# Turning the layer norms by VectorE and DMA instead of TensorE in a macaron transformer block

## The chip, the core and the metric

The kernel runs on one core of a Trainium2 chip. The core has a matrix engine (TensorE, PE in the profile; its weight loads are PEld), a vector engine (VectorE, DVE), a scalar engine (ScalarE, ACT), GpSimd (POOL) and SyncE (SP), which here issues most of the DMAs. Every engine works through its own list of instructions in order and waits for semaphores where it needs another engine's result. The metric is the time of one execution on the device in microseconds; lower is better.

## The reference

The input x is 2 sequences of 1024 rows with 1024 features. Three residual steps follow each other: half a feed-forward layer, an attention layer, and the same half feed-forward layer again, each of them applied to a layer norm of x.

```python
x = x + 0.5 * ffn(layernorm(x))        # gate_w, base_w, base_b, lora_A, lora_B
x = x + attn(layernorm(x))             # Wq, Wk, Wv, Wo
x = x + 0.5 * ffn(layernorm(x))        # the same weights as the first
```

`layernorm` subtracts the mean of a row and divides by its standard deviation. `ffn(h)` is `h @ base_w.T + base_b` plus a low-rank part: 8 experts of rank 16, of which each row uses the best 2 by `h @ gate_w.T`, with softmax weights. `attn(h)` has 32 query heads and 8 key/value heads of width 32, rotary positions, a causal mask and a softmax in fp32, and ends in `ctx @ Wo`.

## The kernel before

The 2048 rows are cut into 16 tiles of 128 rows, eight for each sequence. A tile passes five kinds of stages: a1 (first feed-forward), a2 (queries, keys, values), the attention itself in units of one tile and one key/value head, c1 (output projection) and c2 (second feed-forward). Python generators (`stage_a1`, `stage_a2`, `stage_c1`, `stage_c2`) emit the dense work in pieces, and `step(s)` mixes the pieces of several tiles with the attention units of tile s by a table written by hand (`NORMAL`, `SEQS`). The order in which the instructions finally stand on each engine is then set by a scheduler that plays the program against a timeline of its own.

Matrix products are made at more than fp16 precision by splitting both sides into a high and a low fp16 half; `dense` multiplies high by high, high by low and low by high (lines L406, L407, L408). Its left side must have the features on the partitions, but a layer norm works with rows on the partitions. So every layer norm ends with a turn (a transpose) of a 128 by 1024 tile into `c.tt`, which holds 8 blocks of the high half and 8 of the low half. There are three layer norms for each tile, 48 in all.

`layernorm(xt, turn)` takes the statistics on VectorE, and then ScalarE writes the normalised tile `xn` in fp32 (L397). With `turn=True`, `turn_rows` transposes the fp32 tile by eight TensorE transposes and splits it on the way out of PSUM; that holds for the first two layer norms of the tiles 0 to 2, six cases. In the other 42 cases `turn_halves` first makes the high half on ScalarE (L355) and the low half on VectorE (L357), each 128 by 1024 fp16 in `hl`, and puts two closures into the list `later`. Each closure calls `turned8`: eight TensorE transposes of 128 by 128 into one of the three PSUM buffers `s` (L332), and a copy to `c.tt` on ScalarE (L333). `tick()` is called once for each slot of attention (one block of keys for one head, `unit_s2`); it counts the entries down and runs the first one that is due, `TLAG` slots after it was put there. If a consumer comes earlier, `dense` calls `tt.settle()`, which runs what is left at once.

The same three buffers `s` hold the scores of the first pass (L649, with their maxima on VectorE, L666), and `turned8` also turns queries and keys. The second pass makes the scores again (L782), ScalarE takes the exponential (L788), and TensorE forms the sums with the values (L727).

SP issues in one order: the streamed weights (`prefetch`, 1 MB each, `ws<-wstr`, L418) into three buffers, the rows of maxima that go into the queries (four small DMAs for each pair of heads, `qt<-mt`, L685), the inputs and the outputs (L136, L821). GpSimd issues the DMA that adds the bias to `xt` (L444), once `xn` has been read from it.

Of the kernel before, what the change touches and what calls it, by code (L numbers as in the profile page):

```python
# [9 lines left out]
FP = mybir.dt.float32  # L10
HP = mybir.dt.float16
I32 = mybir.dt.int32
AF = mybir.ActivationFunctionType
ALU = mybir.AluOpType
# [3 lines left out]
NH, NKV, DH, GRP = 32, 8, 32, 4  # L18
E, R = 8, 16
P = 128  # L20
KB = D // P
NT = B * T // P
# [5 lines left out]
LATE = TPB  # L28
# [5 lines left out]
NEARLY = 3  # L34
LOFF = 2
NTURN, NTURN2 = 3, 3
TLAG = 12
SB, LB = 3, 2


# [1 line left out]
def kernel(  # L42
# [16 lines left out]
    nc = tc.nc  # L59
# [5 lines left out]
    small = ctx.enter_context(tc.tile_pool(name="small", bufs=SB))  # L65
    xp = ctx.enter_context(tc.tile_pool(name="xp", bufs=5))
    fpool = ctx.enter_context(tc.tile_pool(name="f32", bufs=1))
    hlp = ctx.enter_context(tc.tile_pool(name="hl", bufs=2))
    tp = ctx.enter_context(tc.tile_pool(name="tp", bufs=4))
    dram = ctx.enter_context(tc.tile_pool(name="dram", bufs=1, space=bass.MemoryType.DRAM))  # L70
    p_dense = ctx.enter_context(tc.tile_pool(name="p_dense", bufs=2, space=bass.MemoryType.PSUM))
# [16 lines left out]
        out=cmask, in_=cmask, compare_op=ALU.is_ge, fill=-NEG, base=0,  # L88
# [6 lines left out]
        out=tri, in_=tri, compare_op=ALU.is_gt, fill=0.0, base=0,  # L95
# [8 lines left out]
    MR = 3 * DH  # L104
    MC = 2
    W = DH
    G = P // W
# [15 lines left out]
    xts, Ts = {}, {}  # L123
# [203 lines left out]
    def turned8(out, src, rows):  # L327

        ps = p_s1.tile([P, GRP, P], FP, name="s1").rearrange("p h k -> p (h k)").bitcast(HP)
        ps = ps.rearrange("p (b q) -> p b q", q=P)  # L330
        for b in range(8):
            nc.tensor.transpose(ps[0:rows, b, :], src[:, b, 0:rows], ident16)  # L332
        nc.scalar.copy(out, ps[0:rows])  # L333

    later = deque()
# [4 lines left out]
    def tick():  # L340
# [3 lines left out]
        if later and later[0][0] <= 0:  # L344
            do_later()

    def turn_halves(xn):

        c = Halves()
        hl = hlp.tile([P, 2 * KB, P], HP, name="hl")  # L350
        for n in range(2):
            h = hl[:, n * KB : (n + 1) * KB, :]
            hi = hl[:, 0:KB, :].rearrange("p k c -> p (k c)")
            if n == 0:
                nc.scalar.copy(hi, xn)  # L355
            else:
                nc.vector.tensor_tensor(h.rearrange("p k c -> p (k c)"), xn, hi, ALU.subtract)  # L357

            def turn(n=n, h=h):
                turned8(c.tt[:, n * KB : (n + 1) * KB, :], h, P)  # L360
                c.todo -= 1

            c.todo += 1
            later.append([TLAG + n, turn])
        return c

    def turn_rows(xn):
# [11 lines left out]
    def layernorm(xt, turn=False):  # L379
        st = small.tile([P, 2, 6], FP, name="bst")  # L380
        for c in range(2):
            nc.vector.bn_stats(st[:, c, :], xt[:, bass.ts(c, 512)])  # L382
        mv = small.tile([P, 2], FP, name="mv")
        nc.vector.bn_aggr(mv, st.rearrange("p a b -> p (a b)"))
        ve = small.tile([P, 1], FP, name="ve")
        nc.gpsimd.tensor_scalar(ve, mv[:, 1:2], EPS, None, ALU.add)
        r = small.tile([P, 1], FP, name="r")
        nc.gpsimd.tensor_tensor(r, ve, mhalf, ALU.pow)
        n1 = small.tile([P, 1], FP, name="n1")
        nc.vector.scalar_tensor_tensor(n1, ve, r, r, ALU.mult, ALU.mult)  # L390
        nc.vector.tensor_scalar(n1, n1, -0.5 * XS, 1.5 * XS, ALU.mult, ALU.add)
        rs = small.tile([P, 1], FP, name="rs")
        nc.vector.tensor_tensor(rs, n1, r, ALU.mult)
        nb = small.tile([P, 1], FP, name="nb")
        nc.vector.scalar_tensor_tensor(nb, mv[:, 0:1], -1.0, rs, ALU.mult, ALU.mult)
        xn = fpool.tile([P, D], FP, name="xn")
        nc.scalar.activation(xn, xt, AF.Identity, bias=nb, scale=rs)  # L397
        return turn_rows(xn) if turn else turn_halves(xn)

    def dense(ps, tt, wsel, n=512, last=True):  # L400
# [11 lines left out]
    turn = [2]  # L412
# [221 lines left out]
    def unit_s1(t, g):  # L634

        b0 = t - t % TPB
        L = t - b0 + 1
        odd = g % 2
        if not odd:
            Ts["mx"] = small.tile([P, 2, TPB, GRP], FP, name="mx", bufs=1)  # L640
        mx = Ts["mx"]
        q = Ts["q1", (t, g - odd)][:, odd * GRP : (odd + 1) * GRP, :]
        for j in reversed(range(L)):
            ps = p_s1.tile([P, GRP, P], FP, name="s1")
            diag = j == L - 1
            off = diag and L > LOFF
            pem = diag and not off
            for h in range(GRP):
                nc.tensor.matmul(  # L649
                    ps[:, h, :], lhsT=q[0 : 3 * DH, h, :], rhs=KT[b0 + j][0 : 3 * DH, g, :],  # L650
                    start=(not pem or h == 0), stop=not pem,
                )
            if pem:
                nc.tensor.matmul(
                    ps, lhsT=negid, rhs=cmask.unsqueeze(1).to_broadcast([P, GRP, P]),
                    start=False, stop=True,
                )
            if off:
                sm = pp.tile([P, GRP, P], FP, name="sm", bufs=1)
                nc.scalar.copy(sm, ps)  # L660
                nc.gpsimd.affine_select(  # L661
                    out=sm, in_=sm, compare_op=ALU.is_ge, fill=-3.0e38, base=0,
                    pattern=[[0, GRP], [-1, P]], channel_multiplier=1,
                )
                ps = sm
            nc.vector.tensor_reduce(mx[:, odd, j, :], ps, AX.X, ALU.max)  # L666
            yield
        if not odd:
            return
        q1 = Ts.pop(("q1", (t, g - 1)))  # L670
        if L > 1:
            m = small.tile([P, 2, GRP], FP, name="m4")
            nc.vector.tensor_reduce(m, mx[:, :, 0:L, :].rearrange("p a j h -> p a h j"), AX.X, ALU.max)
        else:
            m = mx[:, :, 0, :]

        mm = mms[g // 2 % 2]
        mi = mm[:, 0 : 4 * GRP].rearrange("p (i a h) -> p i a h", i=2, a=2)
        nc.vector.tensor_scalar(mi[:, 0], m, 1.0 / MROW, None, ALU.mult)
        nc.vector.scalar_tensor_tensor(mi[:, 1], m, 1.0 / MROW, mi[:, 0], ALU.mult, ALU.subtract)  # L680
        mt = small.tile([P, W], HP, name="mt")
        nc.vector.transpose(mt, mm)
        row = q1[MR : MR + MC].rearrange("i h (a r) -> i a h r", r=W)
        for a in range(G):
            nc.sync.dma_start(out=row[:, a], in_=mt[a * W : a * W + 4 * GRP])  # L685
        Ts["q2", t, g - 1] = q1

    pend = deque()
# [109 lines left out]
    def stage_c1(t):  # L798
        while t not in CT:
            av_batch()  # L800
        tt = CT.pop(t)
        xt = xts[t]
        for n in range(2):
            ps = p_dense.tile([P, 512], FP, name="pd")
            yield from dense_streamed(ps, tt, 3 + n)
            c = bass.ts(n, 512)
            nc.vector.scalar_tensor_tensor(xt[:, c], ps, S["uo", n], xt[:, c], ALU.mult, ALU.add)
            if n == 0:
                yield True
        Ts["x3", t] = layernorm(xt)  # L810
        yield True

    def stage_c2(t):
# [312 lines left out]
```

## Time and profile before

| | |
|---|---|
| time before, median of 3 runs | 1580.93 us (1577.99 to 1581.23) |
| time of the profiled execution | 1578.13 us |
| its span, first to last instruction | 1576.3 us |
| mean granted clock of TensorE | 0.983 |
| busy: TensorE, VectorE, ScalarE, GpSimd | 94%, 71%, 57%, 24% |
| transposes of layer norm halves, L332 | 672 |
| their copies out of PSUM, L333 | 84 of 1019 ns |
| moved by DMA | 214.25 MB, mean 136 GB/s |

A line of the groups reads: line of the kernel, engine, operation, tile written and tiles read, shapes and count; then the busy time of the group in us and the mean of one in ns; then the engine's idle time just before, and what ended it. Busy time counts overlapping instructions once. A matmul's duration is its latency from start to end; the next one can start long before that.

### The profile page before, as it was taken

The numbers are of one execution on the slowest core, as the hardware profiler recorded it, in microseconds if no ns is written. First come the engines' busy times: TensorE is split into PE (matmuls) and PEld (weight loads), VectorE is DVE, ScalarE is ACT, GpSimd is POOL, SyncE is SP. The second block draws the span as 40 slices with busy tenths as digits, with TensorE's granted clock in tenths as the row PEclk, the third lists the DMA queues.
The fourth block names the chain that finished last, engine by engine and source line by source line (L and its number), as shares of the span: only waits on it lengthen the run. The fifth ranks groups of instructions, "written<-read, shape, count | busy, mean of one in ns | idle before, by whom it ended". The sixth has DMA issues, their size and how long they took to land.

```text
span 1576.3 us, 38332 instructions
## 1 busy us (share of the span) xinstructions
PE 1488.0 (94%) x15908; PEld 865.4 (55%) x15908; DVE 1120.9 (71%) x2454; ACT 893.6 (57%) x1523; POOL 381.0 (24%) x636
## 2 busy tenths in 40 slices
PE   5898999999999999989999898999999999999998
PEld 3345556555565555656554454655555556566644
DVE  6777668757587686787744575766869688689653
ACT  8575546556466465565642545554746556566731
POOL 3342333222132231221211122222222122221120
PEclk9998999999999999999999999999999999999999
DMA  8943163262522603513526324345170431601241
GB/s 292 327 134 135 55 227 109 70 249 57 216 95 91 232 14 122 189 42 138 188 76 251 121 95 161 122 156 167 44 277 17 181 129 31 248 27 69 82 161 41
DMA packets 57501, 214.25 MB, mean 136 GB/s; under 512 B 19952, under 2 KB 23024, under 8 KB 37872
## 3 DMA queue, kind: packets, MB, share of 16 engines
q1 hardware_dynamic: 51248, 184.54, 32.6%
q0 software_dynamic: 4640, 16.78, 5.8%
q10 hardware_dynamic: 1440, 10.49, 1.6%
q8 instruction: 125, 2.05, 0.5%
q14 instruction: 48, 0.39, 0.1%
HBM read 191.34 MB, written 20.19 MB: 134 GB/s over the span
## 4 chain that ended last, share of the span: by engine, by line
PE 74%; DVE 11%; ACT 7%; issue 2%; DMA 2%; POOL 1%; SPq 0%; DVEq 0%; ACTq 0%; POOLq 0%
PE pd L406 14%; PE pd L407 14%; PE pd L408 14%; PE av L727 11%; PE s L782 6%; PE s L649 6%; DVE mx L666 3%; PE s L332 3%; ACT p L788 2%; DVE bst L382 1%; DMA ws<-wstr 1%; DVE pair L706 1%; DVE o L736 1%; ACT tt L333 1%; DVE ws L208 1%
## 5 line engine op out<-in xcount | busy, mean ns | idle before, releaser
L788 ACT ACTIVATE p<-s,cs 128x512 f32<-128x512 f32 x576 | 378.0, 690 | 163.5 <-PE s L782 160.8
L666 DVE TENSOR_REDUCE mx<-s 128x4 f32<-128x512 f32 x480 | 313.9, 674 | 80.1 <-PE s L649 70.3
L706 DVE TENSOR_TENSOR pair<-p,p 128x512 f32<-128x512 f32 x256 | 178.9, 701 | 80.9 <-ACT p L788 31.4
L782 PE MATMUL s<-qt,kts 98*128 98x512 f16 x576 | 207.4, 387 | 16.8 <-ACT p L788 9.5
L649 PE MATMUL s<-kts,qt 96*128 96x128 f16 x2304 | 210.3, 223 | 11.2 <-DVE mx L666 8.3
L406 PE MATMUL pd<-ws,tt 128*128 128x512 f16 x544 | 206.4, 380 | 2.5 <-DMA ws<-wstr 1.0
L649 PEld LDWEIGHTS <-qt 96*128 96x128 f16 x2304 | 161.4, 99 | 85.4 <-issue 39.9
L407 PE MATMUL pd<-ws,tt 128*128 128x512 f16 x544 | 206.1, 379 | 0.0
L408 PE MATMUL pd<-ws,tt 128*128 128x512 f16 x544 | 205.3, 379 | 0.0
L406 PE MATMUL pd<-wb,tt 128*128 128x512 f16 x512 | 197.8, 386 | 6.3 <-DVE xt L493 4.9
L407 PE MATMUL pd<-wb,tt 128*128 128x512 f16 x512 | 197.1, 385 | 1.3 <-DVE wb L208 1.3
L408 PEld LDWEIGHTS <-tt 128*128 128x128 f16 x1312 | 128.7, 98 | 125.9 <-issue 7.8
L407 PEld LDWEIGHTS <-tt 128*128 128x128 f16 x1312 | 129.5, 99 | 122.3 <-issue 14.3
L408 PE MATMUL pd<-wb,tt 128*128 128x512 f16 x512 | 196.4, 384 | 0.0
L406 PEld LDWEIGHTS <-tt 128*128 128x128 f16 x1312 | 129.0, 99 | 122.1 <-issue 11.3
L727 PE MATMUL av<-p,va 128*32 128x128 f32 x4608 | 167.2, 278 | 5.1 <-POOL p L790 3.8
L727 PEld LDWEIGHTS av<-p,va 128*32 128x32 f32 x4608 | 115.2, 110 | 74.4 <-issue 50.7
L743 POOL TENSOR_TENSOR tt<-o,tt 128x128 f16<-128x128 f32 x128 | 61.3, 479 | 372.3 <-ACT tt L742 366.0
L790 POOL TENSOR_SCALAR_AFFINE_SELECT p<-p 128x512 f32<-128x512 f32 x128 | 82.6, 647 | 260.4 <-ACT p L788 256.4
L736 DVE RECIPROCAL o<-o 128x128 f32<-128x128 f32 x128 | 120.5, 942 | 22.9 <-ACT o L734 22.7
L661 POOL TENSOR_SCALAR_AFFINE_SELECT sm<-sm 128x512 f32<-128x512 f32 x96 | 71.1, 741 | 229.0 <-ACT sm L660 218.6
L333 ACT COPY tt<-s 128x1024 f16<-128x1024 f16 x84 | 84.3, 1019 | 34.3 <-PE s L332 33.8
(203 smaller groups left out, 2175.0 us busy)
## 6 DMA issues: line engine op xcount, KB each, us to landing
ws<-wstr SPq DMA_DIRECT2D x142, 1024.0 KB
xt<-hb POOLq DMA_DIRECT2D x32, 512.0 KB, 5.5
wstr<-ws ACTq DMA_DIRECT2D x9, 1024.0 KB
xt<-in_x_dram SPq DMA_DIRECT2D x16, 512.0 KB
out_dram<-xt SPq DMA_DIRECT2D x15, 512.0 KB
qt<-mt SPq DMA_DIRECT2D x256, 1.0 KB
ws<-in_wb_dram SPq DMA_DIRECT2D x2, 1024.0 KB
qst<-in_wb_dram SPq DMA_DIRECT2D x2, 1024.0 KB
```

Of the source, the lines that this page charges most:

```text
L333: nc.scalar.copy(out, ps[0:rows])
L406: nc.tensor.matmul(ps, lhsT=th, rhs=wh, start=(k == 0), stop=False)
L407: nc.tensor.matmul(ps, lhsT=th, rhs=wl, start=False, stop=False)
L408: nc.tensor.matmul(ps, lhsT=tl, rhs=wh, start=False, stop=(last and k == KB - 1))
L649: nc.tensor.matmul(ps[:, h, :], lhsT=q[0 : 3 * DH, h, :], rhs=KT[b0 + j][0 : 3 * DH, g, :], start=(not pem or h == 0), stop=not pem,)
L666: nc.vector.tensor_reduce(mx[:, odd, j, :], ps, AX.X, ALU.max)
L706: nc.vector.tensor_tensor(sums, us[i][1], us[i + 1][1], ALU.add)
L727: prev = nc.tensor.matmul(av[rows, i, :], lhsT=w, rhs=p32[:, h, :], start=(us[0][0] == 0 and n == 0), stop=(last and n == len(runs) - 1), ...
L736: nc.vector.reciprocal(rc, rc)
L782: ins = nc.tensor.matmul(ps.rearrange("p h k -> p (h k)"), lhsT=KT[b0 + j][0 : MR + MC, g, :], rhs=q[0 : MR + MC].rearrange("p h k -> p (h ...
L788: nc.scalar.activation(p32, ps, AF.Exp, scale=cs)
L790: nc.gpsimd.affine_select(out=p32, in_=p32, compare_op=ALU.is_ge, fill=0.0, base=0, pattern=[[0, GRP], [1, P]], channel_multiplier=-1,)
```

## The change

Forty of the layer norms are no longer turned by TensorE. VectorE transposes `xn` in fp32, once, in blocks of 32 by 32: inside each group of 32 partitions, 32 rows and 32 features change places. That leaves the rows' groups (`a`, four of them) on the wrong side, and four DMAs, one for each group of 32 partitions, spread 32 partitions of 4 KB over 128 partitions of 1 KB (`xc[:, a]` from `xb[a*32:(a+1)*32]`). For the features to land in order, ScalarE writes `xn` with its features permuted (`xo`, `xi`). The high and the low half are formed from `xc` after the move, directly into `c.tt`, by one ScalarE copy and one VectorE subtraction, as one entry of `later` that is due after 5 slots (`TLAG`) where the two turns were due after 12 and 13. `xb` and `xc` have one buffer each; `hl` is gone. The helper `moved` issues the four DMAs on SP, and the rows of maxima use it too, with the same DMAs as before. The layer norms after attention of tile 15 and tile 8 (`NT - 1` and `LATE`) now go through `turn_rows`. Queries and keys are turned by `turned8` as before.

```diff
-TLAG = 12
+TLAG = 5
...
+    def moved(out, src, rows=W):
+
+        for a in range(G):
+            nc.sync.dma_start(out=out[:, a], in_=src[a * W : a * W + rows])
+
     def turn_halves(xn):
 
         c = Halves()
-        hl = hlp.tile([P, 2 * KB, P], HP, name="hl")
-        for n in range(2):
-            h = hl[:, n * KB : (n + 1) * KB, :]
-            hi = hl[:, 0:KB, :].rearrange("p k c -> p (k c)")
-            if n == 0:
-                nc.scalar.copy(hi, xn)
-            else:
-                nc.vector.tensor_tensor(h.rearrange("p k c -> p (k c)"), xn, hi, ALU.subtract)
-
-            def turn(n=n, h=h):
-                turned8(c.tt[:, n * KB : (n + 1) * KB, :], h, P)
-                c.todo -= 1
-
-            c.todo += 1
-            later.append([TLAG + n, turn])
+        xb = fpool.tile([P, G, KB, W], FP, name="xb")
+        nc.vector.transpose(xb.rearrange("p b k r -> p k b r"), xn.rearrange("p (k b c) -> p k b c", b=G, c=W))
+        xc = fpool.tile([P, G, KB, W], FP, name="xc")
+        moved(xc, xb)
+        hi, lo = [
+            c.tt[:, n * KB : (n + 1) * KB, :].rearrange("p k (a r) -> p k a r", r=W) for n in range(2)
+        ]
+        xk = xc.rearrange("p a k r -> p k a r")
+
+        def halves():
+            nc.scalar.copy(hi, xk)
+            nc.vector.tensor_tensor(lo, xk, hi, ALU.subtract)
+            c.todo = 0
+
+        c.todo = 1
+        later.append([TLAG, halves])
         return c
...
         xn = fpool.tile([P, D], FP, name="xn")
-        nc.scalar.activation(xn, xt, AF.Identity, bias=nb, scale=rs)
+        xo, xi = xn, xt
+        if not turn:
+            xo = xn.rearrange("p (k b c) -> p k c b", b=G, c=W)
+            xi = xt.rearrange("p (k c b) -> p k c b", b=G, c=W)
+        nc.scalar.activation(xo, xi, AF.Identity, bias=nb, scale=rs)
         return turn_rows(xn) if turn else turn_halves(xn)
...
-        row = q1[MR : MR + MC].rearrange("i h (a r) -> i a h r", r=W)
-        for a in range(G):
-            nc.sync.dma_start(out=row[:, a], in_=mt[a * W : a * W + 4 * GRP])
+        moved(q1[MR : MR + MC].rearrange("i h (a r) -> i a h r", r=W), mt, 4 * GRP)
...
-        Ts["x3", t] = layernorm(xt)
+        Ts["x3", t] = layernorm(xt, turn=t in (NT - 1, LATE))
```

More of the change, by code (lines that the diff above doesn't have):

```diff
@@ L67 @@
     fpool = ctx.enter_context(tc.tile_pool(name="f32", bufs=1))
-    hlp = ctx.enter_context(tc.tile_pool(name="hl", bufs=2))
     tp = ctx.enter_context(tc.tile_pool(name="tp", bufs=4))
```

## The prediction

> **What bounds the kernel now.** I read the page's busy shares and chain first, then the groups by line, then TensorE's timeline around one turned tile, the windows of 50 us, and last SP's own issues and waits.
>
> ```profile
> span 1576.3 us, 38332 instructions
> PE 1488.0 (94%) x15908; PEld 865.4 (55%) x15908; DVE 1120.9 (71%) x2454; ACT 893.6 (57%) x1523; POOL 381.0 (24%) x636
> PE 74%; DVE 11%; ACT 7%; issue 2%; DMA 2%; POOL 1%; SPq 0%; DVEq 0%; ACTq 0%; POOLq 0%
> ```
>
> TensorE is busy for 94% of the span and carries 74% of the chain that ended last. What leaves its queue is worth something; what is added elsewhere counts only where it makes TensorE wait.
>
> ```profile
> L333 ACT COPY tt<-s 128x1024 f16<-128x1024 f16 x84 | 84.3, 1019 | 34.3 <-PE s L332 33.8
> L397 ACT ACTIVATE xn<-xt,nb,rs 128x1024 f32<-128x1024 f32 x48 | 59.6, 1243 | 39.1 <-DVE nb L395 32.5 <-DVE hl L357 4.5 <-DVE rs L393 2.0
> L357 DVE TENSOR_TENSOR hl<-xn,hl 128x1024 f16<-128x1024 f32 x42 | 56.5, 1346 | 21.1 <-ACT hl L355 21.0
> L332 PE MATMUL s<-ident,hl 128*128 128x128 f16 x672 | 52.0, 222 | 2.2 <-ACT sm L660 0.9 <-DVE mx L666 0.6 <-ACT tt L742 0.3
> L355 ACT CAST hl<-xn 128x1024 f16<-128x1024 f32 x42 | 43.9, 1046 | 0.5
> L682 DVE STREAM_TRANSPOSE mt<-mm 128x32 f16<-128x32 f16 x64 | 13.0, 203 | 1.3
> ```
>
> These are what the change touches: 42 layer norms, each with 16 transposes on TensorE and two copies out of PSUM on ScalarE. A mean of 222 ns is not what a transpose costs TensorE, because matmuls overlap. The timeline says what it costs: start to next start.
>
> ```profile
> 606.39 0.61 PE L332 MATMUL s<-ident,hl 128*128 128x128 f16 x8
> 606.84 0.39 PE L649 MATMUL s<-kts,qt 96*128 96x128 f16 x4
> 607.06 0.61 PE L332 MATMUL s<-ident,hl 128*128 128x128 f16 x8
> 607.51 0.60 PE L782 MATMUL s<-qt,kts 98*128 98x512 f16 x2
> ```
>
> Eight transposes hold the queue for 0.45 us (606.39 to 606.84, 607.06 to 607.51): 56 ns each, 0.9 us for one layer norm.
>
> ```profile
> 500.00:550.00 50.00, 50.00 (x518) 27.61 (x515) 33.97 (x68) 26.11 (x46) 10.88 (x18) 1.00 0.69 242
> 650.00:700.00 50.00, 45.40 (x622) 28.61 (x623) 44.40 (x92) 32.51 (x55) 12.69 (x20) 0.97 0.21 62
> 1400.00:1450.00 50.00, 50.00 (x769) 33.26 (x768) 45.32 (x92) 33.39 (x59) 9.04 (x14) 0.97 0.11 37
> ```
>
> Columns: busy time of PE, PEld, DVE, ACT, POOL, granted clock, DMA share, GB/s. In most windows TensorE is alone near 50 of 50 and DMA is heavy; where a tile has many keys (650 to 700, 1400 to 1450) VectorE is at 44 to 45 of 50 as well, and DMA is nearly idle.
>
> ```profile
> SPq L685 <- DVE mt L682: 360.0, 43, 24.2
> SPq L418 <- PE pd L408: 280.9, 73, 12.0
> L685 SPq DMA_DIRECT2D qt<-mt x256: 597/610/2811, 121.6 to 1504.7; - x128
> L418 SPq DMA_DIRECT2D ws<-wstr x142: 319/320/453, 118.8 to 1530.7; - x142
> 582.45 1.65 DMA qt<-mt
> 1049.06 4.91 DMA ws<-wstr
> ```
>
> SP issues in order and mostly waits: for VectorE's row of maxima (L685) and for TensorE to free a weight buffer (L418). An issue takes 0.32 us (simple shape) or 0.61 us (three dimensions). The chain has small DMAs at 1.65 us from issue to landing, and runs through a weight load for all its 4.91 us: such a load can arrive just in time.
>
> **The change part by part.** The built order of the two kernels has 40 layer norms in the new form, two (tiles 15 and 8 after attention) moved to the older fp32 form of TensorE, six as before.
>
> *TensorE.* Removed: 42 x 16 x 56 ns = 37.6 us. Added: 2 x 8 fp32 transposes at 8.1/48 = 0.17 us (busy time and count of the group L373 s<-ident,xn), 2.7 us. Net -34.9. The Trainium skill's page TensorE: Matmul & The Clock Gate (Part 4: PE-mode transpose) gives some 275 ns for one in a kernel's context; by that 42 x 16 would be 185 us of queue, and the run would end near 1395. The row's 222 ns agrees with it only as a latency; the starts stand 56 ns apart, and the group's whole busy time is 52.0 us. I take the row.
>
> *The end.* The last layer norm goes xn 1547.4, halves, 16 transposes at 1556.5, copies to 1559.2, and TensorE idles 0.9 us there; the older form is ready sooner. -1.5 us.
>
> *ScalarE.* 84 copies go (-84 us of busy time), the 40 copies for the high half stay (1.05 us each, now read from xc). xn is written with a stride of 32 elements; no row shows such a write. Bounds: 1.24 us as now, or twice that; I take 1.24, as the same count of elements passes. At twice, 40 x 1.24 = 50 us still leave ScalarE below 57%: nothing on the path but POOL's bias add behind xn (L444).
>
> *PSUM.* Turned tiles took 84 turns of the three s buffers that scores (L649), maxima (L666) share. Fewer turns should help, but the scheduler also places everything else anew: -10 to +5 us; I take 0 and keep both ends for the range.
>
> *VectorE.* Added: 40 fp32 transposes of 128x1024. The trace has only fp16 of 128x32, 203 ns, nearly all start-up (32 of them would be 6.5 us). From below, a pass of the same size on the same engine, L357, 1.22 us in the end of the run, 49 us in all. From above, the page VectorE: DVE Perf Modes of the skill (The three transpose paths) states 311 ns for a 128x128 in 32 by 32 blocks at bf16; eight are 2.49 us, 100 us in all. I take 1.25 us: every 512- and 1024-wide pass of this trace runs at 1.2 to 1.4 ns an element, whatever it computes. In the two thirds of the run where VectorE is under 40 of 50 this is hidden. In the crowded windows, some 12 layer norms, 15 us (30 by the rule) come where 5 us of 50 are free; I charge a third, +5 (+10 by the rule).
>
> *SP and the new wait.* Four DMAs for each: 160 issues at 0.32 to 0.61 us, 1.3 to 2.4 us for a set, then 1.65 us to landing; 512 KB in a ring that moves 1 MB in 4.9 us, so about 2.3 us of it. From xn to usable halves: 1.24 + 1.25 + about 1.9 + 1.65 + 1.05 + 1.22 = 8.3 us, against 1.24 + 1.05 + 1.22 + two of 0.45 + two of 1.02 = 6.5 before, if nothing is late. Slots are 2.7 us on average (576 exponentials in 1576 us), under 2 us in crowded steps: five slots are 8 to 14 us, enough on average. But in the built order about a quarter of the 40 have no exponential between xn and the high half: their consumer forces them early. There the high half waits on ScalarE, behind it exponentials (TensorE's s has two buffers for L782), and the low half waits on VectorE, behind it the maxima. Ten times two layer norms stand under 8 us apart (475.2 and 480.4, 578.2 and 585.4, ...), and xb and xc have one buffer: the second one's transposes wait for the first one's DMAs, its DMAs for the first one's halves. I charge 10 x 0.5 = +5. Behind a set in SP's order there stands a weight load 11 times, a row of maxima 18 times, an output 9 times. Delay of up to 2.3 us against loads that are sometimes just in time: 20 x 0.3 = +6. From both sides: 0, if slots cover all, and 40 x 1.5 = +60, if each set makes one load late by what it occupies less the slack.
>
> Sum: -34.9 - 1.5 + 5 + 5 + 6 = -20.4 us on the profiled execution's own 1578.13 (span 1576.3): 1557.7. The median of the runs is 2.8 above that execution: 1560.5.
>
> **The rivals.**
> (a) The freed time is kept whole, or with the PSUM turns: -36 to -48, 1533 to 1545, centre 1540. For it: 84 fewer turns, 84 us less on ScalarE. Against: the single buffers. 17%.
> (b) VectorE becomes the bound of the crowded windows: the 12 layer norms there lose TensorE's gain (12 x 0.9 = 10 us) and pay their transposes in full, 15 us at 1.25, 30 by the page: -36.4 + 10 + 15 + 11 = 0, 1581, or +15, 1596. For it: 45.32 of 50; against: 29% idle overall. 14%.
> (c) Slower: SP's queue. A set cannot be issued before the previous halves have read xc; SP stands, and the weight load or row of maxima behind it stands too; TensorE then waits at L406 or L782 for a DMA. It decides from 0.9 us a layer norm (36.4/40); at 1.5 us it is -36.4 + 60 = +23.6, about 1604. For it: the chain's weight loads at 4.9 to 5.5 us without slack; against: the older kernel already stands 360 us at L685 and TensorE idles only 5.4 us before L782 for the row of maxima (qt<-mt). 22%.
> That the change doesn't do what it says: halves at five slots are only so where no consumer forces them; where that holds for a quarter, it is in the sum.
>
> **How the numbers follow.** The likeliest, 47%, is -20.4: 1560.5, its own range 1548 to 1572. Faster by over 0.2% (3 us, about what a measurement of this kernel can tell from no change): 0.47 + 0.17 + a fifth of (b), 0.67. Slower: 0.22 and two fifths of (b), 0.27. Within: 0.06. The range 1534 to 1592 leaves out the best of (a) and the worse half of (c), about two in ten.
>
> **What would show it.** L332 with hl gone and its 672; TensorE's busy time down by 40 to 50; VectorE's transposes (xb<-xn) near 1.25 us (at 2.5 the VectorE row was wrong); ScalarE near 850 or below; the wait of the high half (tt<-xc) for DMA xc<-xb under 60 us in total; TensorE's idle time before L406 and L782 by DMA still under 20 us. If that last is over 40, rival (c) holds; if the crowded windows grew while the others shrank, (b).

## The result and the profile after

The changed kernel takes 1591.75 us (median of 4 runs, 1588.01 to 1593.46), the kernel before 1579.59 us beside it (1577.99 to 1581.23). The ratio is 1.0073, 95% interval 1.0054 to 1.0092: about 12 us slower, where 20 us faster was forecast. The profiled execution of the changed kernel took 1588.01 us, with a span of 1586.3.

The page of the changed kernel, its head and the chain by engine:

```profile
span 1586.3 us, 37211 instructions
PE 1466.8 (92%) x15252; PEld 832.0 (52%) x15252; DVE 1166.9 (74%) x2496; ACT 851.1 (54%) x1441; POOL 378.3 (24%) x636
PE 55%; DVE 20%; DMA 8%; ACT 7%; issue 4%; SPq 4%; POOL 1%; DVEq 0%; ACTq 0%; POOLq 0%
```

Before, TensorE carried 74% of the chain that ended last; now it is 55%, and VectorE, DMA and SP's queue have taken the rest. TensorE's busy time fell by only 21 us (1488.0 to 1466.8), and its idle time (span less busy) grew from 88.3 to 119.5 us. So work left TensorE and waiting came in its place. Its mean granted clock also fell, from 0.983 to 0.972.

The groups of the changed kernel for the parts that the change adds (busy, mean ns, then the engine's idle time before them):

```profile
L406 ACT ACTIVATE xn<-xt,nb,rs 128x1024 f32<-128x1024 f32 x48 | 97.2, 2025 | 33.1 <-DVE nb L400 30.4 <-DVE nv L458 1.3 <-DVE sm L474 0.7
L355 DVE STREAM_TRANSPOSE xb<-xn 128x1024 f32<-128x1024 f32 x40 | 49.6, 1240 | 31.4 <-ACT xn L406 29.0 <-ACT lg L456 1.4 <-DMA xc<-xb 1.0
L365 DVE TENSOR_TENSOR tt<-xc,tt 128x1024 f16<-128x1024 f32 x40 | 48.8, 1220 | 34.3 <-ACT tt L364 33.9 <-issue 0.2
L364 ACT CAST tt<-xc 128x1024 f16<-128x1024 f32 x40 | 41.8, 1046 | 65.9 <-DMA xc<-xb 62.9 <-DMA ws<-wstr 3.0
```

The transposes with `hl` are gone (L331 is left with queries and keys). VectorE's transpose costs what was taken for it, 1.24 us. The normalisation on ScalarE does not: its mean rose from 1243 to 2025 ns over all 48 (the median of its duration is 2177 ns). ScalarE now stands 62.9 us for the landing of the four DMAs, and VectorE 33.9 us behind ScalarE. Each engine works through its list in order, so what stands behind such a wait stands too.

Where this reaches TensorE, the list of waits of the changed kernel says (in all, times, longest):

```profile
PE s L658 <- DVE mx L675: 15.8, 30, 2.0
PE s L789 <- DMA qt<-mt: 13.8, 11, 2.3
PEld L415 <- ACT tt L364: 12.7, 6, 3.9
PE pd L415 <- ACT tt L364: 10.3, 5, 3.5
```

L789, L658 and L415 are the old L782, L649 and L406. In the kernel before, the first of these waits was 8.3 us (`PE s L649 <- DVE mx L666`) and the second 5.4; the last two are new. Each line is some us; no single wait of TensorE makes up the loss. The windows of 50 us show where much of it lies (busy PE, PEld, DVE, ACT, POOL, clock, DMA share, GB/s):

```profile
550.00:600.00 50.00, 39.46 (x447) 24.08 (x446) 41.30 (x92) 24.80 (x41) 9.54 (x17) 0.83 0.16 33
700.00:750.00 50.00, 45.26 (x483) 26.45 (x483) 37.89 (x71) 25.62 (x44) 7.75 (x13) 0.87 0.36 104
1400.00:1450.00 50.00, 49.07 (x713) 32.90 (x711) 45.37 (x92) 31.90 (x57) 9.06 (x15) 0.90 0.09 34
```

The first two of these windows in the kernel before:

```profile
550.00:600.00 50.00, 46.94 (x605) 29.46 (x602) 42.86 (x95) 32.15 (x53) 13.39 (x18) 0.93 0.06 13
700.00:750.00 50.00, 49.95 (x614) 30.86 (x616) 36.65 (x71) 28.45 (x49) 7.05 (x13) 1.00 0.35 120
```

VectorE is not fuller than before in the fullest window (45.32 before, 45.37 now at 1400).

Of the 40 moved layer norms, 18 stand alone in the trace and 22 form 11 close pairs, in which the second `xn` starts before the first low half has ended. From the start of `xn` to the end of the low half, one that stands alone takes 12.7 us in the median, the first of a pair 13.9 and the second 17.8. Of ScalarE's 62.9 us, 41.7 stand before those that are alone and 18.2 before second ones. TensorE idles more around both kinds: in the stretches from 3 us before `xn` to 22 us after its start, it idles 32.3 us around ten pairs (all but the one of the start-up), where 17.7 before, and 29.4 us around twenty single layer norms, where 15.9 before. So the loss is not that of the close pairs alone.

One close pair, in the first of the windows; the timeline of the changed kernel (start, length, engine):

```profile
583.85 1.25 DVE L355 STREAM_TRANSPOSE xb<-xn 128x1024 f32<-128x1024 f32 x1
...
585.13 2.16 ACT L406 ACTIVATE xn<-xt,nb,rs 128x1024 f32<-128x1024 f32 x1 [0.69 <-DVE sm L474]
585.14 2.56 SPq L349 DMA_DIRECT2D xc<-xb  x4
...
587.58 0.95 POOL L453 DMA_DIRECT2D xt<-hb  x1 [2.24 <-ACT xn L406]
587.62 1.28 DVE L675 TENSOR_REDUCE mx<-s 128x4 f32<-128x512 f32 x2
587.75 0.69 SPq L349 DMA_DIRECT2D qt<-mt  x1
...
589.02 0.68 DVE L675 TENSOR_REDUCE mx<-s 128x4 f32<-128x512 f32 x1
...
589.73 0.25 DVE L682 TENSOR_REDUCE m<-mx 128x8 f32<-128x56 f32 x1
589.94 1.25 DVE L355 STREAM_TRANSPOSE xb<-xn 128x1024 f32<-128x1024 f32 x1
...
590.79 1.05 ACT L364 CAST tt<-xc 128x1024 f16<-128x1024 f32 x1
...
592.68 1.04 PE L789 MATMUL s<-qt,kts 98*128 98x512 f16 x2 [2.34 <-DMA qt<-mt]
592.82 1.21 DVE L365 TENSOR_TENSOR tt<-xc,tt 128x1024 f16<-128x1024 f32 x1
...
594.05 2.49 SPq L349 DMA_DIRECT2D xc<-xb  x4
```

The first layer norm's four issues take SP 2.56 us. The second `xn` is done at 587.29, but its transpose starts at 589.94. VectorE is not idle in these 2.7 us: maxima stand before the transpose in its list. (In the whole run it idles 1.0 us for the one buffer of `xb`.) The second tile's own DMAs start at 594.05, 2.9 us after its transpose and right after the first low half has ended at 594.03: this is the one buffer of `xc`. In 9 of the 11 pairs the second set starts 0.03 us after the first low half; in all 11 together the sets start 28.6 us after their transposes.

The last of four maxima DMAs (587.75) had been put behind the set in SP's order, and TensorE waits for it. The chain that ended last, in order of time:

```profile
587.10 0.61 SPq L349
...
587.75 4.88 DMA qt<-mt
...
592.68 1.04 PE s L789 x2
593.71 0.43 PE pd L415
...
598.39 0.22 PE pd L415
```

The small DMA lands after 4.88 us, where the chain of before had 1.65 us. By the packets of the trace, the set before it has moved its last one at 589.44; from 589.46 to 593.29 the 16 DMA engines carry the bias add that GpSimd issued at 587.58 (`xt<-hb`, 128 packets of 4 KB), and the small DMA's 16 packets of 64 bytes come between these, from 589.91 to 592.15. The bias add goes with slower sets, too: in 15 of the 40 sets its packets move while SP issues, and the four issues then take 3.65 to 4.08 us; in 23 of the other 25 they take 2.49 to 3.56. No run took the bias add away, so its share of the loss is not known.

Matmuls that start 0.22 us apart at 598.39 start 0.43 us apart at 593.71. The windows say since when (columns as above), first of the changed kernel, then two of the kernel before:

```profile
575.00:580.00 5.00, 3.08 (x81) 2.08 (x70) 5.00 (x17) 0.80 (x3) 1.08 (x2) 1.00 0.02 3
580.00:585.00 5.00, 2.87 (x24) 2.21 (x25) 5.00 (x14) 2.77 (x3) 0.69 (x2) 0.53 0.00 0
594.00:596.00 2.00, 2.00 (x6) 0.69 (x5) 0.84 (x3) 0.59 (x2) 0.00 (x0) 0.50 0.27 50
598.00:600.00 2.00, 2.00 (x13) 1.06 (x12) 0.00 (x0) 0.74 (x2) 0.00 (x0) 1.00 0.07 18
...
580.00:585.00 5.00, 3.60 (x28) 2.12 (x28) 5.00 (x13) 1.88 (x5) 2.12 (x2) 0.54 0.01 1
590.00:595.00 5.00, 5.00 (x85) 3.47 (x84) 2.78 (x5) 4.05 (x6) 0.00 (x0) 1.00 0.29 57
```

VectorE is full from 575 on and TensorE thin, and the granted clock falls to a half at 580, in both kernels and before the first set is issued. The kernel before has the full clock again by 590, the changed one, with TensorE still waiting, only by 598.

### The profile page after: what moved, and what is told of

It is laid out like the page before. It is cut to its first block, busy times and chain, and to the rows that moved or that the text cites. A ratio compares the mean times of both kernels' runs of the same rounds, so it can differ in the third digit from the quotient of the medians.

```text
span 1586.3 us, 37211 instructions
## 1 busy us (share of the span) xinstructions
PE 1466.8 (92%) x15252; PEld 832.0 (52%) x15252; DVE 1166.9 (74%) x2496; ACT 851.1 (54%) x1441; POOL 378.3 (24%) x636
## 4 chain that ended last, share of the span: by engine, by line
PE 55%; DVE 20%; DMA 8%; ACT 7%; issue 4%; SPq 4%; POOL 1%; DVEq 0%; ACTq 0%; POOLq 0%
PE pd L415 11%; PE pd L417 10%; PE pd L416 10%; PE av L734 9%; DVE mx L675 6%; PE s L789 6%; PE s L658 4%; SPq L349 4%; DMA xc<-xb 4%; ACT xn L406 2%; DVE pair L713 2%; DMA ws<-wstr 2%; DVE o L743 2%; DVE xb L355 2%; DVE bst L387 2%
## 5 line engine op out<-in xcount | busy, mean ns | idle before, releaser
L658 PE MATMUL s<-kts,qt 96*128 96x128 f16 x2304 | 212.7, 225 | 25.7 <-DVE mx L675 15.8
L789 PE MATMUL s<-qt,kts 98*128 98x512 f16 x576 | 207.8, 391 | 22.3 <-DMA qt<-mt 13.8
L658 PEld LDWEIGHTS <-qt 96*128 96x128 f16 x2304 | 163.4, 100 | 106.3 <-issue 56.1
L415 PE MATMUL pd<-ws,tt 128*128 128x512 f16 x544 | 207.4, 381 | 10.4 <-DMA ws<-wstr 7.0
L415 PE MATMUL pd<-wb,tt 128*128 128x512 f16 x512 | 200.1, 391 | 5.4 <-DVE xt L502 5.4
L415 PEld LDWEIGHTS <-tt 128*128 128x128 f16 x1312 | 130.0, 99 | 138.6 <-issue 15.9
L416 PEld LDWEIGHTS <-tt 128*128 128x128 f16 x1312 | 130.2, 99 | 136.5 <-issue 28.6
L416 PE MATMUL pd<-wb,tt 128*128 128x512 f16 x512 | 199.6, 390 | 1.4 <-DVE wb L207 1.4
L417 PE MATMUL pd<-wb,tt 128*128 128x512 f16 x512 | 199.7, 390 | 0.0
L797 POOL TENSOR_SCALAR_AFFINE_SELECT p<-p 128x512 f32<-128x512 f32 x128 | 88.3, 693 | 222.2 <-ACT p L795 216.9
L406 ACT ACTIVATE xn<-xt,nb,rs 128x1024 f32<-128x1024 f32 x48 | 97.2, 2025 | 33.1 <-DVE nb L400 30.4
```

Of the source, the lines that this page charges most:

```text
L406: nc.scalar.activation(xo, xi, AF.Identity, bias=nb, scale=rs)
L415: nc.tensor.matmul(ps, lhsT=th, rhs=wh, start=(k == 0), stop=False)
L416: nc.tensor.matmul(ps, lhsT=th, rhs=wl, start=False, stop=False)
L417: nc.tensor.matmul(ps, lhsT=tl, rhs=wh, start=False, stop=(last and k == KB - 1))
L658: nc.tensor.matmul(ps[:, h, :], lhsT=q[0 : 3 * DH, h, :], rhs=KT[b0 + j][0 : 3 * DH, g, :], start=(not pem or h == 0), stop=not pem,)
L789: ins = nc.tensor.matmul(ps.rearrange("p h k -> p (h k)"), lhsT=KT[b0 + j][0 : MR + MC, g, :], rhs=q[0 : MR + MC].rearrange("p h k -> p (h ...
```

## Experiments

All kernels stand against the kernel before on the same chip (its medians lie between 1579 and 1582 us); "us" below is (ratio - 1) x 1580 where no median is named. They go from taking the whole turn away to putting its parts back. The scheduler builds the order of the instructions anew for each kernel, so most of them differ in that order as well as in the edit. In the traces, the run with the permutation in the read alone has the changed kernel's order on TensorE, VectorE and ScalarE; the runs without a turn, without DMAs and with the unread move do not. How much an order does by itself was not measured; in the kernel before, `TLAG` alone moved the time by 14 to 15 us (below).

### The parts of the sum

**No turn at all.** `xb`, `xc` and the four DMAs are gone, `xn` is written plainly, and the halves are formed from it:

```diff
-        xk = xc.rearrange("p a k r -> p k a r")
+        xk = xn.rearrange("p (k a r) -> p k a r", a=G, r=W)
```

> The changed kernel with nothing in place of the turn: the halves are formed straight from xn after five slots (the turn of 40 layer norms is left out, and xn is written plainly). It tells what TensorE's relief is worth with nothing paid for it. Theory (the change lost on the latency of its four DMAs): 1530 to 1550 us, about 35 to 45 under the kernel before. Rival (the 672 transposes were not on the path, since other engines set the pace): 1570 to 1580, no gain. Rival (VectorE's transposes eat it): as the theory here, 1530 to 1550.

Measured: 1512.94 us, ratio 0.9573 (0.9558 to 0.9588), -67 us.

```profile
span 1508.3 us, 36919 instructions
PE 1434.8 (95%) x15252; PEld 825.6 (55%) x15252; DVE 1121.8 (74%) x2456; ACT 820.9 (54%) x1441; POOL 375.0 (25%) x636
```

TensorE's busy time is 53 us below before (1488.0 to 1434.8) and its idle time 15 us (88.3 to 73.5). The turn on TensorE, with the 84 copies on ScalarE and the 84 turns of the buffers `s` that went with it, was thus dearer than its 672 starts at 56 ns: what left was nearly twice the 34.9 us of the sum.

**VectorE's transpose and the permuted `xn`, no DMAs.** The halves are formed from `xb`:

```diff
-        moved(xc, xb)
-        xk = xc.rearrange("p a k r -> p k a r")
+        xk = xb.rearrange("p a k r -> p k a r")
```

> The changed kernel without its four DMAs: VectorE transposes and ScalarE's permuted xn stay, the halves are formed from xb (the move between partitions is left out). Theory (DMA latency): within 10 us of the run without any turn, 1540 to 1560, and 30 to 50 under the changed kernel. Rival (VectorE's 1.25 us for each of 40 in crowded windows): 1575 to 1590, little under the changed kernel.

Measured: 1531.76 us, 0.9690 (0.9678 to 0.9703): 18.5 us above the kernel with no turn. The transposes and the slower `xn` were not parted. Much of it lies where the pairs are: around the ten of them, in the same stretches as above, TensorE idles 25.8 us, and 14.0 with no turn.

**The DMAs made, and not waited for.** As the changed kernel, all four DMAs of each set issued and moved, but the halves read `xb`:

```diff
-        xk = xc.rearrange("p a k r -> p k a r")
+        xk = xb.rearrange("p a k r -> p k a r")
```

> The changed kernel with its four DMAs issued as they are, but the halves are formed from xb and nobody reads xc (the move is made, its result is left unused). It parts the waiting for the landing from what the DMAs do to SP and to the other transfers. Measured so far: 1531.8 us without the DMAs, about 1591 with them. Theory now (ScalarE and VectorE stand in their order at the halves until the move has landed): 1532 to 1548. Rival (four issues of 0.6 us on SP and the 0.5 MB delay weights and maxima): 1570 to 1590.

Measured: 1536.25 us, 0.9721 (0.9691 to 0.9751): the issues on SP and 20 MB of traffic cost 5 us, give or take 5. In the source the changed kernel differs from this one only in what the halves read. That costs 1.0073 - 0.9721, 56 us, give or take 6: the waiting for the landing and what hangs on it. Two things hang on it. `xc` comes free only when the halves have been read, and the order built is another: a median of 4 exponentials stand between `xn` and the high half there, and 2 here. The page of this run:

```profile
span 1534.1 us, 37208 instructions
PE 1443.1 (94%) x15252; PEld 826.3 (54%) x15252; DVE 1158.0 (75%) x2496; ACT 853.1 (56%) x1441; POOL 381.4 (25%) x636
```

**Only the two layer norms by the older form**, in the kernel before (`turn=t in (NT - 1, LATE)`):

> The kernel before with only one part of the change: the layer norms after attention of tiles 15 and 8 go by turn_rows. Expected from the prediction's term for the end of the run: 1.5 us less, 1577 to 1580; within what can be told from no change.

Measured: 1581.74 us, 1.0011 (1.0002 to 1.0020). That part brings nothing at the end; it costs about 2 us (0.3 to 3.2).

### What makes the landing dear

**An eighth of the bytes**, in the same four DMAs (`out=xc[:, a, 0:1]`, the rest of `xc` left at zero):

> The changed kernel with the same four DMAs and waits, but each moves an eighth of its bytes (one of eight feature blocks, 128 B to a partition, the rest of xc keeps its zeros). If the transfer of 0.5 MB is the cost (bandwidth, weights behind it): 1545 to 1560. If the cost is the four issues and the landing's fixed time: 1580 to 1592.

Measured: 1613.45 us, 1.0207 (1.0174 to 1.0239). Fewer bytes did not make it faster, which speaks against bandwidth as the cost. Why it became slower than the full move is open: the pieces are then 128 bytes, and the order built is another.

**One DMA instead of four**, from partition to the same partition, the same 512 KB, the regrouping left out:

```diff
-        moved(xc, xb)
+        nc.sync.dma_start(out=xc, in_=xb)
```

> The changed kernel with one DMA of all 512 KB from xb to xc, partition to partition, in place of four (the regrouping over partitions is left out); the halves wait for it as before. SP issues one simple DMA of about 0.33 us instead of four of 0.61. If the four issues in a row (2.4 us of the path, and of SP) are a main part: 1550 to 1570. If it is the landing whatever the number: 1578 to 1590.

Measured: 1570.40 us, 0.9935 (0.9915 to 0.9955), 22 us below the changed kernel. An issue takes 0.54 us, the four 2.5 to 5.3 us; in the trace, `xn`'s start to the end of the low half is 12.0 us in the median against 13.9. ScalarE's wait for the landing did not fall: 62.3 us against 62.9. A shorter path goes with a shorter time although the wait in front of ScalarE stays the same, so that wait's length is not the measure of what the path costs.

**The DMAs from GpSimd**, with the permutation in the read of `xt`:

> The changed kernel with its four DMAs issued by GpSimd instead of SP, and xn written plainly. If what stands behind the moves in SP's order (weights, maxima) is the cost: 1550 to 1570. Theory (the halves wait for the landing): the wait for xc stays at 60 us or grows, since an issue on GpSimd takes about 0.95 us, and GpSimd's masks come later: 1590 to 1610.

Measured: 1591.47 us, 1.0071 (1.0052 to 1.0090). The time is the same from another queue. TensorE's wait for the row of maxima falls from 13.8 to 6.3 us, and ScalarE's for the landing grows from 62.9 to 83.2. So the order on SP is not the whole cost; what it costs by itself was not parted from the longer wait.

**The permutation in the read alone** (`xn` written plainly, `xt` read with the stride):

> The changed kernel whole, but ScalarE reads x with the permutation (steps of 4 elements) and writes xn plainly, where it read plainly and wrote in steps of 32 elements (xn took 2177 ns instead of 1240). If the slow write is a main cause, xn falls back to 1240 and the time falls by 15 us or more, to 1577 or below. Theory (DMA latency): the path of 14.5 us from xn to the low half falls by 0.9 us only, time falls by 3 to 10 us, 1582 to 1589. If the strided read is as slow as the strided write: 2177 ns and the same time.

Measured: 1590.53 us, 1.0059 (1.0038 to 1.0080). The mean of `xn` is 2075 ns (2025 with the strided write): the strided read is as slow as the strided write. With the order of the instructions unchanged, the time is too.

**Twelve slots instead of five** (`TLAG = 12` in the changed kernel):

> The changed kernel with the halves due 12 slots after the layer norm instead of 5. Theory (ScalarE and VectorE stand at the halves because the DMAs land later than five slots): ScalarE's 63 us of waiting for xc fall under 25 us and the time falls by 5 to 20 us, to 1572 to 1587. Rival (single buffers xb and xc are what couples: later halves hold them longer): the second of two close layer norms waits longer, SP stands behind it, time rises to 1595 to 1610.

Measured: 1593.14 us, 1.0087 (1.0064 to 1.0110), ScalarE's wait still 56.2 us. The number of exponentials between `xn` and the high half stays at 4 in the median: consumers and the scheduler place the halves, not `TLAG`. **Twelve slots with the place held**, by an order that puts the halves behind the latest exponential and maximum:

> The changed kernel with the halves due after 12 slots and held there: an order edge puts the high half behind the last exponential issued so far and the low half behind the last maximum, so that the scheduler can't place them sooner (as built, a median of 6.5 exponentials stand between xn and the high half, against 4 in the changed kernel and in the one with 12 slots alone); xn is written plainly. If the placement too soon is the cause: ScalarE waits for xc under 25 us and 1545 to 1570 us. If the single buffers couple the layer norms: xb and SP wait more, 1585 to 1620.

Measured: 1607.69 us, 1.0161 (1.0136 to 1.0187). Two waits of this run:

```profile
ACT tt L368 <- DMA xc<-xb: 33.1, 9, 5.7
DVE xb L356 <- DMA xc<-xb: 14.6, 6, 4.8
```

ScalarE's wait has halved, and the kernel is slower: a later reader holds `xc` longer, and VectorE's transposes now wait 14.6 us for `xb`, 1.0 before. In this kernel, with its single buffers, pushing the halves back traded one wait for another.

### Halves before the move

**The whole computation with the halves formed from `xb`** and the four DMAs carrying fp16 into the turned tile, which the products then read with a stride:

> The whole computation with the halves formed before the move: VectorE's transpose, then the high half on ScalarE and the low half on VectorE at once from xb (no wait for a DMA), then four DMAs of the same size carry both halves in fp16 straight into tt. Only TensorE's products wait for the landing. TensorE's weights are then read in steps of 16 elements (32 B)[...]; VectorE writes xb in steps of 8 elements. Theory (ScalarE and VectorE standing in order for the landing is what costs the 55 us): as the run whose move nobody waits for, 1536, plus some waits of TensorE: 1540 to 1562, faster than both kernels. Rival (the latency of the path to the products is the cost, wherever it is waited for): 1575 to 1600, with TensorE waiting at L415 for the DMA for 40 us and more. Third: weight loads in steps slow TensorE (98 ns for one so far): above 1600.

Measured: 1593.64 us, 1.0090 (1.0066 to 1.0115). The time is the one expected if the path is the cost, the sign is not: TensorE's matmuls wait 12.6 us for the landing, not 40, and ScalarE 28.4 us for `hx`. Weight loads take 133 ns instead of 99, and VectorE's transpose with its strided output takes 2065 ns. Nothing follows from it alone.

**The same without the new strides**, the regrouping of rows and features left out (each DMA carries 128 KB):

```diff
+        hx = fpool.tile([P, G, 2 * KB, W], HP, name="hx")
+        hi, lo = [hx[:, :, n * KB : (n + 1) * KB, :] for n in range(2)]
+        nc.scalar.copy(hi, xb)
+        nc.vector.tensor_tensor(lo, xb, hi, ALU.subtract)
+        moved(c.tt.rearrange("p j c -> p (j c)").rearrange("p (a j r) -> p a j r", a=G, r=W), hx)
```

> The halves are formed straight from xb, before the move, and the four DMAs then carry fp16 halves (64 KB each partition group x 4, the same 512 KB) into the turned tile; the products read it in plain blocks, so the rows and features stand in a wrong order inside it (left out: the regrouping of the order). No engine but TensorE waits for the landing any more, and no access has a new stride. If the ~55 us of the landing come from ScalarE and VectorE standing in front of xc, this takes them away: 1535 to 1550. If they come from the length of the path from xn to a usable tile, whoever waits, TensorE and the single buffer hx pay the same: 1575 to 1595.

and its **control**, the halves written straight into the tile and no DMA:

> As the kernel with halves formed before the move, but written straight into the turned tile and no DMA made at all (left out: the move between groups of partitions). The control for the other: it differs from it by the four DMAs and their buffer alone. Both theories expect about 1530 to 1540, near the kernel with VectorE's transpose and no DMAs (1531.8).

Measured: 1577.45 us, 0.9993 (0.9973 to 1.0013), against 1540.81 us, 0.9751 (0.9731 to 0.9772). Here the four DMAs cost 38 us, with no engine in front of their landing but TensorE and the writer of `hx`. In the changed kernel they cost 1.0073 - 0.9690, 61 us. So with ScalarE and VectorE out of the way of the landing more than half of the cost remains, and this run fits neither expectation well. The group of the high half says what took its place:

```profile
L358 ACT CAST hx<-xb 128x1024 f16<-128x1024 f32 x40 | 41.8, 1046 | 48.2 <-DMA tt<-hx 35.0 <-DVE xb L355 10.4 <-DVE mx L666 1.4
```

`hx` has one buffer, and ScalarE stands 35.0 us until the previous set has left it, nine times, each time at the second tile of a close pair (4.4 to 5.8 us behind the first).

**Two buffers.** Without VectorE's transpose there is memory for them: the halves are formed from a plainly written `xn` into `hx` with `bufs=2`, and the same four DMAs carry them on.

> No VectorE transpose and xn written plainly: the halves are formed from xn at once into hx, which has two buffers (the memory of xb and xc), and the four DMAs carry them into the turned tile (left out: the turn itself). The kernel without any turn (1512.9) is its control. With one buffer the same four DMAs cost 37 us (1540.8 to 1577.5). If the single buffer made most of that (ScalarE stood 35 us for it), two buffers bring it down: 1515 to 1530. If it is the length of the path to a usable tile, TensorE pays it whatever the buffers: 1540 to 1555.

Measured: 1526.35 us, 0.9649 (0.9624 to 0.9673), 12 us above the kernel with no turn.

```profile
span 1525.7 us, 37257 instructions
PE 1442.6 (95%) x15252; PEld 826.5 (54%) x15252; DVE 1119.3 (73%) x2456; ACT 820.2 (54%) x1441; POOL 377.8 (25%) x636
L357 ACT CAST hx<-xn 128x1024 f16<-128x1024 f32 x40 | 41.9, 1048 | 0.4
```

ScalarE's 48.2 us have become 0.4, and the same DMAs cost 12 us instead of 38. In this kernel the path is also shorter by VectorE's transpose and by the slow `xn` (1.24 + 0.9 us), and its control forms the halves later, after five slots. So the 26 us are not the buffer's alone; but its wait, which was to fall, fell to nothing. Two buffers with the whole turn were not tried: `xb` and two of `hx` take 12 KB of a partition, where `hl` took 8 in the kernel before.

### The other ways to turn, and the kernel before

**All 48 layer norms by the older fp32 form:**

> All 48 layer norms by turn_rows: eight fp32 transposes on TensorE at once, no DMA, no five or twelve slots, VectorE's transposes gone. Against the kernel before it has the same TensorE time (8 at 0.11 us for 16 at 0.056) and one ScalarE copy less for each. If ScalarE's copies of the turned halves and the extra pass (2 us of ScalarE a layer norm) made up much of the 67 us that leaving out the turn gave: 1555 to 1575. If it was TensorE's queue alone: 1575 to 1590.

Measured: 1597.83 us, 1.0113 (1.0099 to 1.0127), above both expectations. Its mean granted clock is 0.968, lower than in the changed kernel (0.972), with no move to wait for. Why was not followed.

**The first feed-forward's layer norms by that form, 27 left to the DMAs:**

> The changed kernel, but the first layer norm of every tile (stage a1) goes by TensorE in fp32 at once (turn_rows), so that two layer norms no longer follow each other within 5 us on the single buffers; 27 are still moved by DMA. If pairs on single buffers are the main cost: most of the 55 us go, 1545 to 1565. If each landing costs alike: 27/40 of 55 stay, and 13/40 of TensorE's relief is given back: 1580 to 1590.

Measured: 1630.28 us, 1.0319 (1.0289 to 1.0349), with a wait of ScalarE for the landing as long as with 40 sets:

```profile
ACT tt L364 <- DMA xc<-xb: 66.3, 23, 5.0
PE s L789 <- DMA qt<-mt: 30.5, 17, 4.1
```

In the trace of this run one close pair is left, and 62.7 of the 66.3 us stand before layer norms that are alone. Taking the pairs away did not take the wait away, so close pairs on single buffers do not explain most of it. The kernel is slower by 39 us than the changed one; what of this is the 13 turns more on TensorE and what the order was not taken apart.

**`TLAG` in the kernel before, 5 and 18 instead of 12:**

> The kernel before with only TLAG 5 instead of 12 (turns on TensorE five slots after the layer norm). If the number of slots matters by itself: slower by 5 to 15 us, since transposes come before their halves are due. If the scheduler's placement decides, as 12 slots in the changed kernel suggested: 1575 to 1585.

> The kernel before with its turns 18 slots after the halves instead of 12. Five slots cost it 15 us. If the delay serves to keep the turns off queues that are not ready, later is no worse: 1572 to 1584. If its consumers force them by then, or the turned tile comes late, 1585 to 1600.

Measured: 1595.35 us, 1.0098 (1.0075 to 1.0120), and 1594.77 us, 1.0089 (1.0072 to 1.0106). Twelve is better than both by 14 to 15 us. Whether the delay itself matters here or the order that is built with it, and why both sides lose, was not followed further. None of the kernels that make the whole computation beats the kernel before.

## Why the prediction was wrong

The signs of the sum's terms were right but for the small one of the end, and three sizes were not. From the runs (ratio differences x 1580; each also holds what a newly built order does):

| term | forecast | by the runs |
|---|---|---|
| the turn off TensorE, the end, PSUM | -36.4 | -67 |
| VectorE's transposes and the permuted `xn` | +5 | +18.5 |
| four issues a layer norm, traffic, SP's order | +6 | +5 |
| waiting for the landing, and what hangs on it | +5 | +56 |
| sum | -20.4 | +12 |

*TensorE.* "42 x 16 x 56 ns" counted only start to next start. In the trace of before, the transposes with what stands behind them hold the queue for 48.2 us; without them TensorE's busy time fell by 53.2 us and its idle time by 14.8. I put the PSUM turns at 0 between -10 and +5. How much of the other 15 us is theirs was not measured by itself. The end was no gain (the run with that part alone: +2). The fp32 transposes were charged at 0.17 us by their busy time; start to next start they are 0.11, which is 0.9 us less in all.

*`xn`.* I took 1.24 us between 1.24 and twice that. It is 2.18, near the upper bound, and on the path of every moved layer norm. "Nothing on the path but POOL's bias add" overlooked that the transpose and all behind it wait for it.

*VectorE.* The row of the trace was right against the page VectorE: DVE Perf Modes of the Trainium skill (The three transpose paths): 1.24 us, where eight 128 by 128 at its 311 ns would be an estimated 2.49. ("1.2 to 1.4 ns an element" is a little narrow: L493 has 739 ns for 512.) What the transposes cost the end was too low: +18.5 with the slow `xn`, nearer to the 25 of rival (b) than to my 5. But the fullest window did not fill further, and the rest of (b), TensorE's gain lost in the crowded windows, is not seen in the kernel without DMAs, which is 49 us faster than the one before.

*The wait: the step that failed.* "I charge 10 x 0.5 = +5" should have been about +56. It priced ten close pairs and took the rest as covered, since five slots were "enough on average". They were not. ScalarE waits for the landing before 26 of the 40 layer norms, and 41.7 of its 62.9 us stand before those that are alone. The halves do not stand where the slots say: 4 exponentials lie between, with `TLAG` 5 and with 12. And the path that was added up at 8.3 us takes 12.7 in the median of those that are alone: `xn` takes 0.9 us more, the four issues 3.8 in the median where 1.9 was taken, most of them while GpSimd's bias add moves, for which the sum had no term, and from the last issue to the landing it is 2.0 to 3.4 us where ScalarE waits for it (6.3 once), not 1.65. Half a microsecond for a pair was too little as well: at 585 us the second set waits 2.9 us for `xc`, and the second tiles' path is 17.8 us in the median.

How the 56 us divide between the standing in order, the one buffer of `xc` and the built order stays open. Two runs bear on the buffers, and they point to different sides: with nearly all pairs gone the wait for the landing was no shorter, while with the halves before the move a second buffer ended ScalarE's 35.0 us of waiting for the first.

The old path took longer still (median about 21 us from `xn` to the last copy in the trace of before), but its steps waited as entries of a list, where now ScalarE, and VectorE behind it, wait in order.

*Where the loss shows.* Idle time of TensorE is +31.2 us. The clock is a second part: (1 - 0.972) x 1586.3 = 44.4 us of full speed are lost against 26.8 before, an estimate of 18 us more. Compared with the busy time of the kernel with no turn, the changed kernel's is 32 us longer for the same 15252 matmuls. Where the DMAs are made and not waited for the clock is 0.985, so it falls with the waits here; but it is 0.968 in the kernel with all layer norms by the older form, which has no such waits.

*Rival (c)* named the right side and nearly the right time (1604), but its mechanism only in part. SP's queue is visible in the close pair; yet the issues alone cost 5 us and GpSimd's queue did no better. TensorE's waits before L415 and L789 by DMA rose from 6.4 us to 20.8 (7.0 and 13.8), just over the 20 that was to hold and far from the 40 that was set as the rival's sign. Two other signs turned: the wait of the high half is 62.9 us, above the 60 that was named, and TensorE's busy time fell by 21 us, not 40 to 50. The size of the high half's wait alone was no measure, as the single DMA showed (same wait, 22 us faster). That the rival's time came out near is in part luck.

## What to carry to other kernels

Before work leaves the busiest engine, add up the new path step by step with what runs beside it (here another queue's transfer), and ask at each step which engine stands in order for it. An average distance between users does not cover the wait. To size such a wait, make the transfers and leave their result unread: here that run put some 56 us on the waiting and what hangs on it, and 5 on the transfers. A wait moved from one engine's list to a buffer is not gone, and its total in the profile does not say what it costs the end. Intermediate tiles with one buffer deserve a run with two, where there is memory.

## What the runs showed of the hardware

- ScalarE writing 128x1024 fp32 in steps of 32 elements takes 2.18 us in the median, reading it in steps of 4 elements 2.23 us, plainly 1.24 us.
- VectorE's fp32 transpose in blocks of 32 by 32 of a 128x1024 tile takes 1.24 us, and 2.07 us where its output is strided.
- TensorE's weight loads of 128x128 fp16 take 99 ns, and 133 ns where the elements lie 16 apart.
- A DMA of 16 packets of 64 bytes took 4.88 us to land behind 512 KB of its own queue and beside 512 KB of GpSimd's, 1.65 us in the chain of before.
- Four issues of 128 KB on SP took 3.65 to 4.08 us where packets of GpSimd's bias add moved meanwhile, mostly 2.5 us otherwise.
- At a granted clock of 0.50 (594 to 596 us) matmuls on 512 columns started 0.43 us apart, at 1.00 (598 to 600 us) 0.22 us.
